# Moving the weights and the tiles of tokens of the projection of k and v to other offsets in SBUF

## The chip, the core and the metric

The kernel runs on one core of one Trainium2 chip. The metric is the device time of one execution in microseconds; three runs of the kernel before gave 2835.35 to 2835.84 us, with a median of 2835.64. The engines named are PE (TensorE, the matrix products) with PEld (its loads of the stationary operand), DVE (VectorE), ACT (ScalarE), POOL (GpSimd) and SP (SyncE, which here only issues transfers).

## The reference

One block of a perceiver: cross-attention to a long context, self-attention with rotary positions, and a feed-forward part with 4-bit weights, each added to its input. What the change touches is the projection of the context to keys and values, over all 8192 context tokens.

```python
def _L0_xattn_ref(x, cond, Wq, bq, Wkv, bkv, Wp, bp):
    B, N, C = x.shape                                   # C = 1024, 16 heads of 64
    q = (x @ Wq + bq).reshape(1, B * N, H, hd)          # 512 queries
    kv = (cond @ Wkv + bkv).reshape(1, -1, 2, H, hd)    # 8192 tokens, 1024 -> 2048
    k, v = (kv[:, :, 0], kv[:, :, 1])
    ...
    q = _fq_sym(q, axis=-1)
    k = _fq_sym(k, axis=-1)
    v = _fq_sym(v, axis=2)
    attn = softmax(q k^T), quantised
    return attn v @ Wp + bp

x = x + _L0_xattn_ref(_layernorm(x), ctx_2048, ...)
x = x + _L0_attn_ref(_layernorm(x), ...)
x = x + _L0_ffn_ref(_layernorm(x), ...)
```

Because k, v and q are rounded to 8 bits, the projection needs nearly all the precision of float32.

## The kernel before

**The products.** A float32 number is split into three tiles of the type float32r: h (high part), l (low part, for weights scaled up) and d (a combination of both). The product of tokens and weights is then h·h and l·l into one PSUM tile `kv_a`, and d·d into another, `kv_b` (`project`, lines 345 to 357). For each tile of 128 tokens there are two halves of 512 output columns, eight blocks k of 128 input channels and three products: 48 matmuls. The tokens are the stationary operand (`lhsT`, 128 x 128, which PEld loads) and the weights the moving one (`rhs`, 128 x 512). Each matmul is preceded by its own load of tokens, and in the trace that load starts 2 to 4 ns after the matmul before has started. The order is fixed: for each half, k from 0 to 7, and in each k the products h, l, d.

**The passes.** There are 64 tiles of tokens, gone through twice: first for v (weights `w3[1]`, s = 0 to 63), then for k (`w3[0]`, s = 64 to 127), 6144 matmuls in all. Beside the pass for v, DVE and ACT also expand the 4-bit weights of the feed-forward part; beside the pass for k, values and keys are quantised and stored. Most of the order of the work is written out by hand: `do(step, function, ...)` puts a function at a step and `perform` issues them in the order of the steps; the middle of the pass for v is a plain loop, which the framework's own scheduler orders. After both passes come the attention to the context (scores, exponentials, values), self-attention, the feed-forward products (line 169 for gate and up, line 1533 for down), all with the same split into h, l and d where float32 precision is needed.

**The tiles.** The weights are 24 tiles of 128 partitions x 1024 numbers (4096 bytes a partition): eight each of `w_h`, `w_l` and `w_d`, in the pool `kv_w` (`weight_hi`, line 240). The tokens of tile s are three tiles of 4096 bytes, `c_h`, `c_l` and `c_d` (`tokens_hi`, line 334), in three sets by s % 3: sets 0 and 2 lie in the pool `early` (`kv_early`), set 1 in the pool `pools["c"]` (`kv_c`). The tiles `bq` (line 277) and `xn` (line 281) of the projection of q use the same places as `c_l2` and `c_h2` before these are needed.

**The addresses.** A pool's places are laid out one after another, in the order in which the program first asks for them, in whole 32 bytes. `kv_w` begins on the left with a tile of 32 bytes at byte 17,024, so the weights begin at 17,056: `w_h` 17,056, 21,152, ..., then `w_l` from 49,824 and `w_d` from 82,592, all 4096 apart and all at 160 modulo 512. After them come three rows of biases (2048 bytes each) and `kv_c` from 121,504: set 1 lies at 160 modulo 512 too. `kv_early` lies on the right and ends at 212,704. Its eleven places of 4096 bytes are `vmax` (167,648), two of `c_raw`, two of `w_raw`, `c_l2` (188,128), `c_h2` (192,224), `c_h0`, `c_l0`, `c_d0` and `c_d2` (208,608): all at 224 modulo 512. A block k of the tokens is 512 bytes further, and the second half of the weights 2048 bytes, so neither changes the place modulo 512.

In the later stages the operands lie as follows, modulo 512: line 1160 has weights (moving) at 448 and stationary tiles at 480; line 1318 moving at 480 and stationary at 448; line 169 moving at 480 and stationary at 128; line 1533 moving at 128 and stationary h, l, d at 160, 160, 128 for the first quarter of a half and at 288, 288, 128 from then on.

Before the change:

Of the kernel before, what the change touches and what calls it, by code (L numbers as in the profile page):

```python
# [34 lines left out]
F32 = mybir.dt.float32  # L35
# [4 lines left out]
F32R = mybir.dt.float32r  # L40
# [6 lines left out]
P = 128  # L47
B, S, C = 4, 128, 1024
NT = B * S // P
NC = C // P  # L50
# [25 lines left out]
REST = (NI - 8 * WHOLE) // 2  # L76
EARLY = 8

LOWEST = -3.0e38
F16_UNITS = 16777216.0  # L80
UP = 4096.0
# [5 lines left out]
def tile_perceiver(  # L87
# [44 lines left out]
    def layernorm(pool, xt, xn, parts=1):  # L132
        st = pool.tile([P, 2, nc.vector.BN_STATS_DIM], F32, name="ln_st", tag="ln_st", bufs=2)
        for i in range(2):
            nc.vector.bn_stats(st[:, i, :], xt[:, ts(i, 512)])
        mv = pool.tile([P, 2], F32, name="ln_mv", tag="ln_mv", bufs=2)
        nc.vector.bn_aggr(mv, st)
        rstd = pool.tile([P, 1], F32, name="ln_rstd", tag="ln_rstd", bufs=2)
        nc.vector.tensor_scalar_add(rstd, mv[:, 1:2], 1e-5)
        nc.scalar.activation(rstd, rstd, AF.Sqrt)  # L140
        nc.vector.reciprocal(rstd, rstd)
        for i in range(parts):
            cols = ts(i, C // parts)
            nc.vector.tensor_scalar(
                xn[:, cols], xt[:, cols], mv[:, 0:1], rstd, ALU.subtract, ALU.mult
            )
# [11 lines left out]
    def split_hi(src, hi):  # L158
        nc.scalar.mul(hi, src, 1.0 - 0.5 / UP)  # L159
# [48 lines left out]
    early = early_s.enter_context(tc.tile_pool(name="kv_early", bufs=2, side="right"))  # L208
# [3 lines left out]
    kv_w = kvstack.enter_context(tc.tile_pool(name="kv_w", bufs=1))  # L212
# [18 lines left out]
    raws, tokens, accs, fs = {}, {}, {}, {}  # L231
# [7 lines left out]

    def weight_hi(i, k):  # L240
        w3[i].append(
            [kv_w.tile([P, C], F32R, name=f"w_{n}", tag=f"w_{n}", bufs=NC) for n in "hld"]
        )
        split_hi(raws["w", i, k], w3[i][k][0])

# [15 lines left out]
    xts, xns, xnTs, qps, qns, wqs, bqs, xpts = {}, {}, {}, {}, {}, {}, {}, {}  # L261
# [12 lines left out]
        queue.dma_start(out=wqs[n, k], in_=wq_src[:, k, ts(n, 512)])  # L274

    def load_bq():
        bqs[0] = early.tile([P, C], F32, name="bq", tag="c_l2", bufs=1)
        nc.sync.dma_start(out=bqs[0], in_=xbq.partition_broadcast(P))

    def norm_of_x(t):  # L280
        xns[t] = early.tile([P, C], F32, name=f"xn{t}", tag="c_h2", bufs=1)
        layernorm(q_t, xts.pop(t), xns[t], parts=2 if t == 0 else 1)

    def transposes_of_x(t):
# [41 lines left out]
    raws, tokens, accs, fs = {}, {}, {}, {}  # L326
# [7 lines left out]
    def tokens_hi(s):  # L334

        pool = pools["c"] if s % 3 == 1 else early
        tokens[s] = [
            pool.tile([P, NC, P], F32R, name=f"c_{n}", tag=f"c_{n}{s % 3}", bufs=1) for n in "hld"
        ]
        split_hi(raws[s], tokens[s][0])  # L340

    def tokens_lo(s):
# [109 lines left out]
    for k in range(NC):  # L452
        do(0.1 if k < 3 else 0.3, load_wq, 0, k)
        do(0.65 if k == 0 else 30, load_wq, 1, k)
    do(0.2, load_x_of_q, 1)
    do(0.45, load_bq)
    do(0.5, load_x_of_q, 2)
    do(0.55, load_x_of_q, 3)
# [3 lines left out]
    for t, at in enumerate((4, 9, 16.4, 24.5)):  # L462
        do(at, norm_of_x, t)
        at = first[t] - (1.6 if t == 0 else 1.9)
        do(at, transposes_of_x, t)
        do(at + 0.1, copies_of_x, t)
        for n, q_at in enumerate(((19, 27.5, 33, 40.9)[t], (48.7, 54.1, 61, 67.5)[t])):
            for k in range(NC):
                do((first, second)[n][t] + 0.88 * k, project_q, n, t, k)
            do(q_at, quantise_q, n, t)  # L470
            do(q_at + 3.1, transpose_q, n, t)
            do(q_at + 8.5, store_q, n, t)
    for k, (raw, hi, lo) in enumerate(
        (
            (0.4, 12.8, 13),
            (0.6, 19.5, 22),
            (16.5, 24, 30.4),
            (24.6, 34, 36),
            (33, 37.5, 38.4),
            (38.5, 42, 43.8),  # L480
            (41, 49.5, 51.6),
            (46.3, 55, 57),
        )
    ):
        do(raw, weight_raw, 1, k)
        do(hi, weight_hi, 1, k)
        do(lo, weight_lo, 1, k)
        do(lo + 2.6, weight_up, 1, k)
    for n in range(2):
        do(27.6, load_tokens, n)  # L490
        do(40, kv_bias, 1, n)
    do(45, tokens_hi, 0)
    do(46.2, tokens_lo, 0)
    do(48.8, load_tokens, 2)
    do(60, lambda: nc.sync.dma_start(out=shifts, in_=nibbles))
    at = 67.4
    for s in range(2):
        for n in range(2):
            for k in range(NC):
                do(at + 11.2 * s + 5.6 * n + 0.7 * k, project, s, n, k)  # L500
    do(at - 0.05, open_pools)
    do(at + 1.5, tokens_hi, 1)
    do(at + 3.2, tokens_lo, 1)
    do(at + 3.3, load_tokens, 3)
    do(at + 6, join, 0, 0)
    do(at + 6.3, tokens_hi, 2)
    do(at + 7.5, tokens_lo, 2)
    do(at + 7.6, load_tokens, 4)
# [177 lines left out]
    for k in range(NC):  # L686
        do(at + (k if k < 4 else 4 * k - 10), weight_raw, 0, k)
        do(at + 4 * k + 4.1, weight_hi, 0, k)
        do(at + 4 * k + 5.7, weight_lo, 0, k)
        do(at + (9.6, 13.4, 17.6, 22.8, 26.6, 30.4, 35, 38.6)[k], weight_up, 0, k)  # L690
# [13 lines left out]
    for u in range(KT):  # L704
        at = TILE * (KT + u)
        s = KT + u
# [50 lines left out]
    with tc.tile_pool(name="at_e", bufs=1) as at_e, tc.tile_pool(  # L757
        name="at_s", bufs=4
    ) as small, tc.tile_pool(name="at", bufs=2) as at, tc.tile_pool(
        name="at_ps", bufs=3, space=PSUM  # L760
# [32 lines left out]
        def scores(n, g):  # L793
# [10 lines left out]
            for i in range(2):  # L804
# [12 lines left out]
                scale=1.0,  # L817
                scalar=LOWEST,
                op0=ALU.mult,
# [4 lines left out]
        def maximum(n):  # L824
# [8 lines left out]
                scale=sqs[:, 1, t, h : h + 1],  # L833
                scalar=-LOWEST,
                op0=ALU.add,
# [174 lines left out]
        with tc.manual_schedule():  # L1010
            for s in range(n_steps + LAG_V):
                n, g = divmod(s, NSC)
# [9 lines left out]
                if n < len(units):  # L1022
                    h, t = units[n]
# [316 lines left out]
    with tc.manual_schedule():  # L1340
# [10 lines left out]
        for h, (w, n) in enumerate(PARTS):  # L1351
            s = PART * h
# [72 lines left out]
        s = PART * len(PARTS)  # L1425
# [12 lines left out]
    with tc.tile_pool(name="ff_t", bufs=2) as ff_t, tc.tile_pool(  # L1438
        name="ff_a", bufs=1
# [36 lines left out]
        with tc.tile_pool(name="ff_g", bufs=2) as ff_g:  # L1476
# [13 lines left out]
            with tc.tile_pool(name="g_ps", bufs=2, space=PSUM) as g_ps, tc.tile_pool(  # L1490
                name="u_ps", bufs=2, space=PSUM
# [17 lines left out]
        with tc.tile_pool(name="ff_h", bufs=1) as ff_h, tc.tile_pool(  # L1509
            name="y_ps", bufs=1, space=PSUM  # L1510
# [135 lines left out]
```

## Time and profile before

| | |
|---|---|
| median of 3 runs | 2835.64 us (2835.35 to 2835.84) |
| profiled execution, first to last instruction | 2844.0 us, 8.4 us above that median |
| mean granted clock of PE | 0.984; 1.00 from 0 to 1350 us |
| PE busy | 2655.8 us, 93% |
| PEld busy | 2060.8 us, 72% |
| DVE busy | 2417.0 us, 85% |
| ACT busy | 1264.9 us, 44% |
| POOL busy | 461.0 us, 16% |
| matmuls of line 351 | 6144, from 66.6 to 1489.2 us |
| one of them, start to end | 387 ns at least, median 393 |
| one load of tokens for them | median 188 ns |

The profile is of one execution; of its time outside the span only the difference to the median is known, and that is negative, so the profile itself costs something. A group's line gives the source line, the engine and operation, the tiles written and read, the shapes, how many there were, their busy time, the mean length of one, and the idle time ahead of them. Matmuls are pipelined, so a group's busy time counts overlap once, while the mean length of one contains it. The view by windows gives for each stretch its length, then for each engine its busy time and how many instructions fall in it, the granted clock (1.00 is full speed), the busy share of the transfers and their rate. The timeline gives for every instruction its start and its length in us.

### The profile page before, as it was taken

The page shows a single profiled execution, that of the slowest core. Times are in us where ns is not written, and L with a number is a line of the kernel's source. Part 1 is how long each engine was busy: PE and PEld are TensorE (multiplying, and loading weights), DVE is VectorE, ACT ScalarE, POOL GpSimd, SP SyncE. Part 2 cuts the span into 40 slices and gives each one's busy share as a digit, 9 for nine tenths or more (in the row PEclk, how much of TensorE's full clock was granted, in tenths as well). Part 3 has the DMA queues.
Part 4 walks back from the last instruction along what each step waited for, and adds up shares of the span by engine and source line. Part 5 has one row for each costly group of instructions (what it writes and reads, how often), then busy time and mean ns, then how long its engine had stood idle before and what let it go on. Part 6 is the DMA issues. An engine that isn't in the chain of part 4 may idle for free.

```text
span 2844.0 us, 41119 instructions
## 1 busy us (share of the span) xinstructions
PE 2655.8 (93%) x15496; PEld 2060.8 (72%) x15496; DVE 2417.0 (85%) x3963; ACT 1264.9 (44%) x1404; POOL 461.0 (16%) x615
## 2 busy tenths in 40 slices
PE   9999999999999999999997877778778899999998
PEld 4888888888888888888874555555555687788887
DVE  7999998555799988888879999999996898776684
ACT  4111121211323333333218999999994244333332
POOL 0111111000012222222122332233312000000000
PEclk9999999999999999999998999999999999999999
DMA  6655565222447776767436898887874221122222
GB/s 198 207 197 195 192 210 200 89 98 95 137 127 202 192 192 182 194 183 188 124 88 143 164 165 164 155 162 152 168 142 146 86 80 61 52 97 97 96 90 96
DMA packets 450327, 412.66 MB, mean 145 GB/s; under 512 B 354888, under 2 KB 359560, under 8 KB 450128
## 3 DMA queue, kind: packets, MB, share of 16 engines
q1 hardware_dynamic: 401984, 249.86, 36.4%
q0 software_dynamic: 47088, 159.12, 17.4%
q8 instruction: 122, 2.00, 0.3%
q10 hardware_dynamic: 1056, 1.05, 0.2%
q14 instruction: 77, 0.63, 0.1%
HBM read 220.14 MB, written 104.34 MB: 114 GB/s over the span
## 4 chain that ended last, share of the span: by engine, by line
PE 73%; DVE 19%; issue 4%; ACT 2%; DMA 1%; POOL 0%; DVEq 0%; SPq 0%; ACTq 0%; POOLq 0%
PE kv_a L351 33%; PE kv_b L351 17%; DVE e L813 14%; PE acc_a L1160 3%; PE gate_a L169 3%; PE up_a L169 3%; PE y_a L1533 3%; PE q_ps L301 2%; PE acc_b L1160 1%; PE up_b L169 1%; PE gate_b L169 1%; PE y_b L1533 1%; PE a_pt L862 1%; PE sc L806 1%; DVE sw_l L162 1%
## 5 line engine op out<-in xcount | busy, mean ns | idle before, releaser
L351 PE MATMUL kv_a<-w_h,c_h 128*128 128x512 f32 x2048 | 806.4, 394 | 0.0
L351 PE MATMUL kv_a<-w_l,c_l 128*128 128x512 f32 x2048 | 806.0, 394 | 0.2 <-ACT w_l L250 0.2
L351 PE MATMUL kv_b<-w_d,c_d 128*128 128x512 f32 x2048 | 806.1, 394 | 0.0
L813 DVE CUSTOM_DVE_ANT_0 e<-sc,sk 128x1024 f32<-128x1024 f32 x512 | 593.7, 1219 | 14.0 <-PE sc L806 13.0
L847 ACT ACTIVATE a<-e,m,sqs 128x4096 int16<-128x4096 f32 x128 | 490.4, 3831 | 25.4 <-DVE m L829 21.9
L351 PEld LDWEIGHTS kv_a<-w_l,c_l 128*128 128x128 f32 x2048 | 384.8, 188 | 89.6 <-ACT w_l L250 0.6
L351 PEld LDWEIGHTS kv_a<-w_h,c_h 128*128 128x128 f32 x2048 | 384.9, 188 | 88.9 <-issue 0.2
L351 PEld LDWEIGHTS kv_b<-w_d,c_d 128*128 128x128 f32 x2048 | 384.8, 188 | 89.0 <-DVE c_d L163 0.3
L159 ACT ACTIVATE c_h<-c_raw 128x1024 fp32r<-128x1024 f32 x128 | 135.5, 1059 | 463.8 <-PE kv_a L351 454.3
L365 DVE SCALAR_TENSOR_TENSOR f<-kv_a,bkv 128x512 f32<-128x512 f32 x256 | 175.8, 687 | 167.0 <-PE kv_a L351 166.3
L806 PE MATMUL sc<-kt,qT 64*128 64x512 bf16 x1024 | 207.6, 398 | 95.0 <-DVE mx L813 93.6
L604 ACT CAST kst<-kT 128x512 bf16<-128x512 int16 x128 | 89.5, 700 | 300.1 <-DMA kT<-ki 300.0
L862 PE MATMUL a_pt<-ident,a 128*128 128x128 f32 x1024 | 177.6, 299 | 25.2 <-ACT a L847 21.0
L366 DVE SCALAR_TENSOR_TENSOR f<-kv_b,f 128x512 f32<-128x512 f32 x256 | 176.7, 690 | 19.0
L786 POOL PARTITION_BROADCAST sk<-sk_row x120 | 142.5, 1298 | 308.2 <-DVE mx L813 308.1
L862 PEld LDWEIGHTS a_pt<-ident,a 128*128 128x128 f32 x1024 | 113.5, 147 | 92.1 <-ACT a L847 51.8
L162 DVE TENSOR_TENSOR fw_l<-fw_raw,fw_h 128x1024 fp32r<-128x1024 f32 x64 | 78.3, 1224 | 99.4 <-ACT fw_h L159 99.3
L806 PEld LDWEIGHTS <-qT 64*128 64x128 bf16 x1024 | 71.6, 93 | 124.1 <-issue 94.2
L162 DVE TENSOR_TENSOR c_l<-c_raw,c_h 128x1024 fp32r<-128x1024 f32 x128 | 155.6, 1216 | 6.6 <-ACT c_h L159 6.1
L163 DVE SCALAR_TENSOR_TENSOR c_d<-c_l,c_raw 128x1024 fp32r<-128x1024 f32 x128 | 156.3, 1221 | 2.3
L159 ACT ACTIVATE fw_h<-fw_raw 128x1024 fp32r<-128x1024 f32 x64 | 67.9, 1061 | 175.0 <-PE y_a L1533 71.5
L571 ACT CAST vq<-vi 128x1024 f16<-128x1024 int16 x64 | 67.1, 1049 | 174.0 <-DVE vi L564 137.1
(214 smaller groups left out, 4121.0 us busy)
## 6 DMA issues: line engine op xcount, KB each, us to landing
c_raw<-in_ctxT SPq DMA_DIRECT2D x128, 512.0 KB, 3.6
v_d<-f POOLq DMA_DIRECT2D x64, 512.0 KB, 3.1
vl<-v_d POOLq DMA_DIRECT2D x64, 512.0 KB, 4.3
gu_d<-w_ffn POOLq DMA_DIRECT2D x44, 512.0 KB, 3.1
fw_raw<-gu_d SPq DMA_DIRECT2D x42, 512.0 KB, 3.2
k_d<-kst POOLq DMA_DIRECT2D x128, 128.0 KB, 3.4
vq_d<-vq POOLq DMA_DIRECT2D x32, 512.0 KB, 5.0
kt<-k_d SPq DMA_DIRECT2D x64, 256.0 KB, 3.8
```

What stands on the lines that cost most here:

```text
L159: nc.scalar.mul(hi, src, 1.0 - 0.5 / UP)
L162: nc.vector.tensor_tensor(lo, src, hi, ALU.subtract)
L163: nc.vector.scalar_tensor_tensor(df, lo, -1.0 - UP, src, ALU.mult, ALU.add)
L169: nc.tensor.matmul(ps, lhsT=lhs(i, k), rhs=rhs(i, k), start=(k == 0 and i != 1), stop=(k == NC - 1 and i != 0),)
L351: nc.tensor.matmul(ps, lhsT=tokens[s][i][:, k, :], rhs=w3[s < KT][k][i][:, ts(n, 512)], start=(k == 0 and i != 1), stop=(k == NC - 1 and i ...
L365: nc.vector.scalar_tensor_tensor(f, a, 1.0 + 1.0 / UP, bias[s < KT][n], ALU.mult, ALU.add)
L366: nc.vector.scalar_tensor_tensor(f, b, -1.0 / UP, f, ALU.mult, ALU.add)
L786: nc.gpsimd.partition_broadcast(tile_of_scales(h, g), sks_at[h][32 * c : 32 * c + 1, ts(half, SC)], channels=P)
L806: nc.tensor.matmul(ps[:, ts(i, 512)], lhsT=qT[rows, h, ts(t, P)], rhs=kts[h, g // 2][rows, ts(g % 2, 512)], start=True, stop=True,)
L813: nc.vector.tensor_tensor_reduce(out=state[n]["e"][-1][:, ts(g % (NSC // NEC), SC)], in0=ps, in1=sks_at[h, g], scale=1.0, scalar=LOWEST, o ...
L847: nc.scalar.activation(a, st["e"][c], AF.Exp, bias=st["m"], scale=sqs[:, 0, t, h : h + 1], accum_out=sums[h][:, t, c : c + 1],)
L862: nc.tensor.transpose(pt[:, i, :], a[:, at_word + P * i : at_word + P * i + P], ident)
```

## The change

The weights' tiles get eight more numbers (32 bytes) per partition, of which the products use the first 1024. The tiles of tokens, and `bq` and `xn`, which share their places, get 72 more numbers in `kv_early` and 16 more in `kv_c`; and the tokens begin inside their tile at a word given by `STARTS` for the set (s % 3) and the part (h, l, d). Number, order and size of all instructions stay.

```diff
+PADS = (72, 16)
+STARTS = ((0, 8, 64), (4, 12, 0), (64, 72, 16))
...
     def weight_hi(i, k):
         w3[i].append(
-            [kv_w.tile([P, C], F32R, name=f"w_{n}", tag=f"w_{n}", bufs=NC) for n in "hld"]
+            [
+                kv_w.tile([P, C + 8], F32R, name=f"w_{n}", tag=f"w_{n}", bufs=NC)[:, :C]
+                for n in "hld"
+            ]
         )
...
-        bqs[0] = early.tile([P, C], F32, name="bq", tag="c_l2", bufs=1)
+        bqs[0] = early.tile([P, C + PADS[0]], F32, name="bq", tag="c_l2", bufs=1)[:, :C]
...
-        xns[t] = early.tile([P, C], F32, name=f"xn{t}", tag="c_h2", bufs=1)
+        xns[t] = early.tile([P, C + PADS[0]], F32, name=f"xn{t}", tag="c_h2", bufs=1)[:, :C]
...
     def tokens_hi(s):
 
         pool = pools["c"] if s % 3 == 1 else early
-        tokens[s] = [
-            pool.tile([P, NC, P], F32R, name=f"c_{n}", tag=f"c_{n}{s % 3}", bufs=1) for n in "hld"
-        ]
+        tokens[s] = []
+        for i, n in enumerate("hld"):
+            pad = PADS[s % 3 == 1]
+            tile_ = pool.tile([P, C + pad], F32R, name=f"c_{n}", tag=f"c_{n}{s % 3}", bufs=1)
+            at_word = STARTS[s % 3][i]
+            tokens[s].append(tile_[:, at_word : at_word + C].rearrange("p (k q) -> p k q", q=P))
         split_hi(raws[s], tokens[s][0])
```

## The prediction

> **What bounds the kernel now.** I read the share of the engines first, then the chain of work that ended last, then the costliest groups.
>
> ```profile
> span 2844.0 us, 41119 instructions
> ...
> PE 73%; DVE 19%; issue 4%; ACT 2%; DMA 1%; POOL 0%; DVEq 0%; SPq 0%; ACTq 0%; POOLq 0%
> ...
> L351 PE MATMUL kv_a<-w_h,c_h 128*128 128x512 f32 x2048 | 806.4, 394 | 0.0
> L351 PE MATMUL kv_a<-w_l,c_l 128*128 128x512 f32 x2048 | 806.0, 394 | 0.2 <-ACT w_l L250 0.2
> L351 PE MATMUL kv_b<-w_d,c_d 128*128 128x512 f32 x2048 | 806.1, 394 | 0.0
> ```
>
> The 6144 matmuls of line 351 hold the chain from 66.6 to 1489.2 us and wait for nothing. The 394 ns is a length with overlap; what counts is the step from one start to the next. The view by windows, over whole tiles of tokens, gives that step (the counts hold one or two matmuls of the neighbour; a tile is 48):
>
> ```profile
> core 0: us, PE busy (x) PEld busy (x), PEclk, DMA share, GB/s
> 288.98:311.37 22.39, 22.39 (x97) 18.04 (x96) 1.00 0.58 206
> 311.37:322.28 10.91, 10.91 (x49) 9.01 (x48) 1.00 0.51 193
> 322.28:344.68 22.40, 22.40 (x98) 18.05 (x96) 1.00 0.52 182
> 344.68:355.59 10.91, 10.91 (x50) 9.01 (x49) 1.00 0.59 216
> ```
>
> Two tiles take 22.39 us, 233.2 ns a step; the third takes 10.91, 227.3 ns a step; then again. The granted clock is 1.00 in all four. The slower two are the sets of tokens with s % 3 of 2 and 0, in kv_early; the faster is set 1, in kv_c. Only addresses tell them apart: weights lie at 160 modulo 512, set 1 at 160 too, sets 0 and 2 at 224. Inside set 1 the steps settle at about 226.7:
>
> ```profile
> 319.79 0.39 PE L351 MATMUL kv_a<-w_l,c_l 128*128 128x512 f32 x1
> 320.01 0.39 PE L351 MATMUL kv_b<-w_d,c_d 128*128 128x512 f32 x1
> 320.24 0.39 PE L351 MATMUL kv_a<-w_h,c_h 128*128 128x512 f32 x1
> 320.47 0.39 PE L351 MATMUL kv_a<-w_l,c_l 128*128 128x512 f32 x1
> 320.69 0.39 PE L351 MATMUL kv_b<-w_d,c_d 128*128 128x512 f32 x1
> 320.92 0.39 PE L351 MATMUL kv_a<-w_h,c_h 128*128 128x512 f32 x1
> ```
>
> Five steps in 1.13 us. While a matmul streams a weights tile, the tokens of the next are loaded; so I take as variable the distance: offset of the next matmul's tokens less offset of this one's weights, modulo 512. Set 1 has 0, sets 0 and 2 have 64. Later stages, by their addresses, add more:
>
> ```profile
> core 0: us, PE busy (x) PEld busy (x), PEclk, DMA share, GB/s
> 2500.46:2523.79 23.33, 23.33 (x101) 18.77 (x100) 1.00 0.31 107
> ...
> 2735.50:2763.23 27.73, 27.73 (x122) 22.54 (x121) 1.00 0.28 96
> ```
>
> The gate and up products (line 169) have 160 throughout: 23.33/100 = 233.3. The products of line 1160 have 32 and those of line 1318 have 480; starts a few matmuls apart in their timelines give 233 there as well. The down products (line 1533) repeat the distances 160, 160, 0: 27.73 us over 120 steps is 231.1, just (2 x 233.3 + 226.7)/3. So four distances other than 0 cost one and the same step, and 0 saves 6.7 ns even standing alone. Earlier in line 1533 the repeat is 32, 0, 32 and a step is 231.9, so mixing can cost 0.8 more.
>
> **The change part by part.** *Weights.* A tile grows by 32 bytes, so the eight of a name lie 32 apart: w_h and w_d at 160 to 384, w_l at 416 round to 128. *Tokens.* Six tiles of kv_early grow by 288 bytes, three of kv_c by 64. kv_early ends at byte 212,704 and grows downwards by 1728; kv_c is moved up by 24 x 32 = 768. With the starts inside, h, l and d lie at 96, 416, 416 (set 0), 432, 16, 32 (set 1), 64, 320, 0 (set 2). Over eight k and three products a set has 24 distances. Of the 72, four are 0 (one, one and two in sets 0, 1, 2); 14 are among 32, 64, 160 and 480; 54 are at distances that no row shows, 16 of them, all in set 1, at odd multiples of 16.
>
> *The step.* Before: 4074 steps beside sets 0 and 2 at 233.3 are 950.5 us, 2059 beside set 1 at 227.3 are 468.0; together 1418.5 over 6133 (the few that wait are left out), a mean of 231.3. For an unseen distance the low end is the fastest step that any row keeps up, 226.7, and nothing but the absence of rows excludes less; the high end is the slowest single step, about 239 (line 1533). I take 233.3: four of four distances that are not 0 have it, on both sides of 0 (480 is -32) and with either tile at several offsets. After: 6133 x 233.3 = 1430.8, less 6133 x 4/72 x 6.7 = 2.3 for the zeros: 1428.5, or **+10.0**. Mixed distances cost between 0 and 6133 x 0.8 = 4.9 by the two stretches of line 1533; I take 2. Sum **+12**, against the profiled execution's 2844.0, which is 8.4 over the median of 2835.64; a difference in PE's steps carries over to either.
>
> *All else is taken at nothing.* Instructions, their shapes and their order stay: views of 1024 elements in longer rows. The splits do not feel the offset: line 162 takes 1206 to 1226 ns over all its tiles, those at 160 and those at 224. bq and xn share tags with c_l2 and c_h2 and are only moved. c_raw lands 3.6 us after issue, tiles ahead; any loss there is covered by PE's 11 us a tile. The keys' tiles of the attention, opened during the last tile of tokens, now lie over other old tiles, some of set 0 where they had been over set 2. Those are read out when the last tile begins, 11 us before PE needs keys, so no wait; uncovered, a load is 3.8 us. A slower PE delays ACT, DVE and the queues by as much and gives each more slack.
>
> *A rule against the change.* Rows: 227.3 and 233.2 for the same shapes at one clock. The Trainium skill, "TensorE: Matmul & The Clock Gate", Step-by-step: what each phase is for, says of PE's two read ports: "Loading the next tile's weights doesn't steal SBUF read bandwidth from the running matmul." By it offsets would be worth nothing and the time would stay at 2835.6; the rows differ, and I go by them. The same page, Back-to-back issue gap, puts 512 columns at N / 2.4 + 2.5 = 215.8 ns, and an estimate from it, were every collision gone, is 6133 x (231.3 - 215.8) = 95 us less; no run here shows such a step.
>
> **The rivals.** *Unseen distances are cheap (faster).* If 0 is no isolated dip and the 54 unseen pairs run at 226.7, PE gains 6133 x 54/72 x 6.7 = 30.8 against 1428.5: 1397.7, -20.8, about 2815. For it: three quarters of the pairs are unseen. Against: both neighbours of 0, a near and a far distance, are equal. It decides once the mean step falls under 231.3, that is once some 22 of the 54 run at 226.7. DVE caps it in part, for it is nearly full while the feed-forward weights are expanded, and 5.2 us of 300 is all that PE could gain there:
>
> ```profile
> 150.00:300.00 150.00, 150.00 (x651) 121.86 (x650) 148.01 (x340) 27.76 (x27) 21.67 (x37) 1.00 0.54 195
> 300.00:450.00 150.00, 150.00 (x650) 121.86 (x649) 146.78 (x244) 29.71 (x28) 26.59 (x39) 1.00 0.59 210
> ```
>
> *Offsets are not the cause, or the period is shorter (no change).* If the pool makes set 1 fast, nothing moves: 2836. Against: line 1533 follows its offsets inside one stage. With a period of 128, ten further pairs count as zeros: 6133 x 10/72 x 6.7 = 5.7 less, 2842, at the edge of no change. *Odd starts or mixing cost extra (slower still).* If the 16 pairs of set 1 at odd multiples of 16 take 240 ns, that is 2059 x 16/24 x 6.7 = 9.2; with full mixing (2.9 more than taken) about 2860. Nothing in the trace shows such a start under a matmul of this kind.
>
> **How the numbers follow.** A fair measurement tells 0.2%, 5.7 us, from no change. The forecast has 0.57, its own range 2843 to 2853. Slower still has 0.13, no change 0.08, faster 0.22. Faster by over 0.2% is thus 0.22, within 0.08, slower 0.70. The range reaches to 2862 above (0.06 left out) and to 2818 below, leaving out about 0.12.
>
> **What would show it.** Right: tiles of set 1 at 11.2 us like the others, no third tile at 10.91; the down products unchanged at 231.1; DVE's busy time unchanged, its idle time longer. In the timeline four pairs in 72 stay near 227, and those name the distance 0. Wrong: if tiles of sets 0 and 2 fall under 11.1 us, unseen distances are cheap; if set 1 alone exceeds 11.3, odd starts cost; if set 1 stays at 10.91, the offset was never the cause.

## The result and the profile after

The changed kernel takes 2843.52 us (median of 10 runs, 2840.78 to 2848.04) against 2836.97 of the kernel before (10 runs, 2833.85 to 2839.90): a ratio of 1.0020, 95% interval 1.0011 to 1.0029, so 3 to 8 us slower. 12 us more than 2835.64 had been forecast, about 2848, with a range of 2818 to 2862.

Engines, chain and costliest groups, from the page of the changed kernel (`project` is now line 359):

```profile
span 2838.9 us, 41119 instructions
...
PE 71%; DVE 21%; issue 5%; ACT 2%; DMA 1%; POOL 0%; DVEq 0%; SPq 0%; POOLq 0%; ACTq 0%
...
L359 PE MATMUL kv_b<-w_d,c_d 128*128 128x512 f32 x2048 | 809.9, 395 | 0.0
L359 PE MATMUL kv_a<-w_l,c_l 128*128 128x512 f32 x2048 | 807.6, 394 | 0.2 <-ACT w_l L255 0.2
L359 PE MATMUL kv_a<-w_h,c_h 128*128 128x512 f32 x2048 | 805.8, 393 | 0.0
```

The three groups still wait for next to nothing (0.2 us), and the names at the head of the chain are the same. Their mean lengths, 393 to 395 ns, tell nothing of the change, because they contain the overlap; the step from start to start has to be read from windows. Here are three tiles of tokens of the second pass, sets 0, 1 and 2 in this order, first before and then after (columns: stretch and its length, PE and PEld busy with their counts, granted clock, share of the transfers, GB/s):

```profile
1067.10:1078.30 11.20, 11.20 (x50) 9.02 (x48) 1.00 0.71 180
1078.30:1089.21 10.91, 10.91 (x50) 9.01 (x49) 1.00 0.63 168
1089.21:1100.41 11.20, 11.20 (x50) 9.02 (x49) 1.00 0.85 229
```

```profile
1072.28:1083.40 11.12, 11.12 (x50) 9.01 (x48) 1.00 0.67 162
1083.40:1094.54 11.14, 11.14 (x49) 9.01 (x48) 1.00 0.63 168
1094.54:1105.72 11.18, 11.18 (x49) 9.02 (x48) 1.00 0.87 220
```

A tile is 48 steps. Set 1 loses the most, from 10.91 to 11.14 us (227.3 to 232.1 ns a step). Sets 0 and 2 gain a little, 233.3 to 231.7 and 232.9. Over all 6134 steps that don't wait (6133 before), the mean is 232.24 ns where it was 231.29.

From the first to the last start the projection takes 1428.2 us instead of 1422.5. **These 5.7 us are the whole of the change**, within what the runs can tell. That the profiled execution is nevertheless shorter than the one before (2838.9 against 2844.0) lies mostly in the attention, which takes 655.1 us from its first score to its last product with the values before and 646.5 after. In the same stretch of it the granted clock was 0.95 before and 0.99 after; whether that is the cause is not shown. The tiles of the keys there do move with the change, by 960 bytes, but two kernels below move them too, by 64 bytes, and their medians differ from before by what their projection differs (24.9 of 24.9 us, and 12.5 of 12.4). So I put the long attention down to that one execution. The 8.4 us by which it exceeds its median are no price of profiling as such either: the changed kernel's profiled execution took 2840.78 us for a span of 2838.9.

```profile
1650.00:1800.00 150.00, 117.67 (x1422) 81.95 (x1421) 143.79 (x281) 141.60 (x121) 47.43 (x54) 0.95 0.87 159
```

```profile
1650.00:1800.00 150.00, 118.55 (x1470) 82.87 (x1469) 148.46 (x291) 145.74 (x123) 49.70 (x56) 0.99 0.83 165
```

So below, stages are compared by their own windows, and spans are not. What should have stayed did: the gate and up products take 23.33 us for 100 steps (lines 169 and 171), and the down products 27.72 us for 120 (27.73 before):

```profile
2495.30:2518.63 23.33, 23.33 (x102) 18.76 (x101) 1.00 0.29 105
...
2730.34:2758.06 27.72, 27.72 (x121) 22.53 (x121) 1.00 0.28 95
```

### The profile page after: what moved, and what is told of

Read it like the earlier page. It is cut to its first block, busy times and chain, and to the rows that moved or that the text cites. A ratio compares the mean times of both kernels' runs of the same rounds, so it can differ in the third digit from the quotient of the medians.

```text
span 2838.9 us, 41119 instructions
## 1 busy us (share of the span) xinstructions
PE 2650.6 (93%) x15496; PEld 2051.6 (72%) x15496; DVE 2416.5 (85%) x3963; ACT 1263.3 (44%) x1404; POOL 462.5 (16%) x615
## 4 chain that ended last, share of the span: by engine, by line
PE 71%; DVE 21%; issue 5%; ACT 2%; DMA 1%; POOL 0%; DVEq 0%; SPq 0%; POOLq 0%; ACTq 0%
PE kv_a L359 33%; PE kv_b L359 17%; DVE e L821 15%; PE up_a L171 3%; PE gate_a L171 3%; PE y_a L1541 3%; PE acc_a L1168 3%; PE up_b L171 1%; PE gate_b L171 1%; PE y_b L1541 1%; PE acc_b L1168 1%; PE q_ps L306 1%; DVE sw_l L164 1%; PE a_pt L870 1%; PE sc L814 1%
## 5 line engine op out<-in xcount | busy, mean ns | idle before, releaser
L164 DVE TENSOR_TENSOR c_l<-c_raw,c_h 128x1024 fp32r<-128x1024 f32 x128 | 155.8, 1218 | 5.8 <-ACT c_h L161 5.5
```

The lines of the kernel that those rows point to most:

```text
L164: nc.vector.tensor_tensor(lo, src, hi, ALU.subtract)
```

## The experiments

The word "distance" is the prediction's: the offset of the next matmul's tokens less that of this one's weights. All kernels below but the last version leave everything outside the projection alone, but for tiles that shift along with its pools, and none leaves out any work. Times are compared with the kernel before as run beside them on the same chip; steps are from the starts in the trace.

### Every distance 0, and every distance 64

The first tile of `kv_w` made 64 bytes longer moves the weights and set 1 to 224 modulo 512, where sets 0 and 2 already lie:

```diff
-    shifts = kv_w.tile([P, 2], I32, name="shifts")
+    shifts = kv_w.tile([P, 18], I32, name="shifts")[:, :2]
```

> The kernel before with its small first tile 64 bytes longer, so that the weights and set 1 lie at 224 modulo 512 like sets 0 and 2: every distance is 0. If the distance sets the step (theory A: 0 is cheap wherever the tiles lie; theory B, each distance has its own price, says the same here), all three sets take 226.7 to 227.3 ns a step and the projection loses 4074 x 6.0 = 24 us; where the expansion of the feed-forward weights fills VectorE up to 2 of these are lost: about 2812 to 2816. If the pool or the region of set 1 makes it fast (theory C), sets 0 and 2 stay at 233.3 and the time at 2836.

The opposite moves set 1 alone, by 64 bytes inside `kv_c` (a longer `c_h1` whose tokens start 16 words in):

```diff
+PADS = ((0, 0, 0), (16, 0, 0), (0, 0, 0))
+STARTS = ((0, 0, 0), (16, 0, 0), (0, 0, 0))
...
+            pad, at_word = PADS[s % 3][i], STARTS[s % 3][i]
+            tile_ = pool.tile([P, C + pad], F32R, name=f"c_{n}", tag=f"c_{n}{s % 3}", bufs=1)
+            tokens[s].append(tile_[:, at_word : at_word + C].rearrange("p (k q) -> p k q", q=P))
```

> The kernel before with set 1 moved by 64 bytes inside its pool, to 224: every distance is 64. Theories A and B: set 1 rises from 227.3 to 233.3 ns a step like the others, 2059 x 6.0 = 12.4 us more, about 2849. Theory C (the pool): set 1 stays at 227.3 and the time at 2836.

Three tiles as above, sets 0, 1, 2; first the kernel with every distance 0, then the one with every distance 64:

```profile
1053.00:1063.88 10.88, 10.88 (x49) 9.01 (x48) 1.00 0.71 184
1063.88:1074.76 10.88, 10.88 (x49) 9.01 (x48) 1.00 0.63 168
1074.76:1085.64 10.88, 10.88 (x49) 9.01 (x48) 1.00 0.89 216
```

```profile
1080.27:1091.46 11.19, 11.19 (x49) 8.97 (x48) 1.00 0.67 173
1091.46:1102.66 11.20, 11.20 (x49) 8.98 (x48) 1.00 0.67 170
1102.66:1113.87 11.21, 11.21 (x50) 8.98 (x49) 1.00 0.85 216
```

All sets at 226.7, or all at 233.3, whichever pool they lie in: addresses make the difference and pools do not. It is also the relation that counts and not the tokens' own place: tokens at 224 take 233.3 beside weights at 160 and 226.7 beside weights at 224. 64 bytes in one tile bring 2813.91 us against 2838.81 (ratio 0.9908, 0.9891 to 0.9924), and the projection takes 1397.7 us, 24.9 less. With every distance 64 it is 2851.27 (1.0044, 1.0029 to 1.0059). VectorE's ceiling in the first pass was reached but held PE up nowhere in it: of the 300 us from 150 on DVE was busy for 299.19, and PE started 26 more matmuls there than before (1327 against 1301). Some 28.4 us were saved in steps, and 3.5 of them went to waits of PE early in the second pass: its steps of over 260 ns add up to 7.5 us where they were 4.0, the longest (2.4 us) while a transpose waits for DVE.

```profile
150.00:300.00 150.00, 150.00 (x663) 124.20 (x662) 150.00 (x345) 29.78 (x28) 22.22 (x38) 1.00 0.57 198
300.00:450.00 150.00, 150.00 (x664) 124.20 (x663) 149.19 (x253) 28.72 (x27) 33.47 (x40) 1.00 0.61 213
```

### The change's two parts alone

The weights alone, with the changed kernel's padding and starts of the tokens set to nothing:

```diff
-PADS = (72, 16)
-STARTS = ((0, 8, 64), (4, 12, 0), (64, 72, 16))
+PADS = (0, 0)
+STARTS = ((0, 0, 0), (0, 0, 0), (0, 0, 0))
```

> The change's weights alone: a weight tile is 32 bytes longer, tokens without padding and without starts of their own (sets 0 and 2 at 224, set 1 at 416, whose tiles follow the weights). Distances run through multiples of 32 with k and are all even multiples of 16. Theory A: no pair but the few at 0 is cheap, 233 ns a step in all three sets, about 2848, unless mixing itself saves steps. Theory B: the mean over the distances' own prices, as in the changed kernel some 232 ns, about 2843.

The tokens alone, with the changed kernel's weights as before:

```diff
-                kv_w.tile([P, C + 8], F32R, name=f"w_{n}", tag=f"w_{n}", bufs=NC)[:, :C]
+                kv_w.tile([P, C], F32R, name=f"w_{n}", tag=f"w_{n}", bufs=NC)
```

> The change's tokens alone: weights at 160 throughout, tokens padded and started as in the change. Each set repeats three distances (set 0: 256, 256, 448; set 1: 112, 128, 16; set 2: 160, 352, 416, for the pairs to l, to d and to the next h), none of them 0. Theory A: 233.3 ns in all sets, 2849. Theory B: sets differ among themselves, each the mean of its three prices; no number can be had from the rows so far. If odd multiples of 16 cost extra, set 1 is the slowest.

| | step of set 0, 1, 2 (ns) | projection (us) | time beside before (us) | ratio, interval |
|---|---|---|---|---|
| before | 233.3, 227.3, 233.3 | 1422.5 | | |
| weights alone | 232.5, 232.5, 232.6 | 1429.7 | 2846.74 and 2838.81 | 1.0024, 1.0014 to 1.0034 |
| tokens alone | 230.9, 232.4, 231.3 | 1424.1 | 2839.99 and 2838.81 | 1.0003, 0.9994 to 1.0012 |
| both: the change | 231.7, 232.1, 232.9 | 1428.2 | 2843.52 and 2836.97 | 1.0020, 1.0011 to 1.0029 |

Spread weights make all sets alike, at 224 and at 416 for the tokens; that alone is 7.2 us of the projection. Tokens at offsets of their own take from set 1 about what they give to sets 0 and 2. Tokens alone never have distance 0 modulo 512 and still stay below 233.3, so the theory that only 0 is cheap is wrong, unless mixing is what saves. That was the next question.

### One distance held at a time

Weights at 160; each set of tokens is brought to one distance by padding, three distances a kernel. The lists of the first kernel, with the code of the kernel for distance 64:

```diff
+PADS = ((0, 0, 64), (64, 0, 0), (64, 0, 48))
+STARTS = ((0, 0, 0), (64, 0, 0), (0, 0, 0))
```

> The kernel before with weights at 160 and each set of tokens at one distance of its own: 128 (set 0), 256 (set 1), 384 (set 2). Theory A (held, every distance but 0 costs the same): 233.3 ns a step in all three sets, some 2850. Theory B (each distance has its own price): the sets differ; since tokens moved alone gave 230.9 in a set with 256, 256 and 448, the distance 256 should then be below 231. A period of 256 would show as set 1 at 226.7, one of 128 as all three at 226.7.

> The same with the distances 16 (set 0), 96 (set 1) and 320 (set 2). Theory A: 233.3 ns a step in all three, and 16 no dearer than 96. Theory B: the sets differ; the single steps of the changed kernel suggest 320 below 230. If the dip at 0 has a width of more than 16 bytes, set 0 stays near 227.

> The same with the distances 48 (set 0), 192 (set 1) and 448 (set 2). Theory A: 233.3 ns a step in all three. Theory B: the sets differ, 448 below 231 by the single steps of tokens alone.

> Weights at 160, one distance held in each set: 480 (set 0), 32 (set 1), 160 (set 2), which so far were seen only in other stages. With a price for each distance and a period of 256, all three are at 233 to 234 ns a step, and the mean of the eight prices is 231.9. If the stage or the shape of the moving operand (lines 169 and 1318 read four separate pieces) matters, they differ from 233.3.

First 128, 256, 384, then 48, 192, 448:

```profile
1066.20:1077.36 11.16, 11.16 (x49) 9.05 (x48) 1.00 0.74 188
1077.36:1088.28 10.92, 10.92 (x49) 9.02 (x48) 1.00 0.60 168
1088.28:1099.44 11.16, 11.16 (x50) 9.05 (x49) 1.00 0.86 209
```

```profile
1065.74:1076.93 11.19, 11.19 (x49) 9.12 (x48) 1.00 0.75 185
1076.93:1087.92 10.99, 10.99 (x50) 9.02 (x48) 1.00 0.67 167
1087.92:1098.91 10.99, 10.99 (x49) 9.02 (x48) 1.00 0.87 197
```

128 and 384 cost the same to 0.2 ns, and so do 192 and 448; 256 settles at 226.7 like 0, after some slow steps at the start of each tile that make its mean 227.4. **The period is 256 bytes and not 512**, nor 128, since 128 costs 232.5 and 0 costs 226.7. All held distances together:

| distance modulo 256 | 0 | 16 | 32 | 48 | 64 | 96 | 128 | 160 | 192 | 224 |
|---|---|---|---|---|---|---|---|---|---|---|
| step, ns | 226.7 | 226.7 or 233.4 | 233.3 | 233.2 | 233.3 | 234.2 | 232.5 | 233.3 | 228.9 | 233.3 |

In the tokens alone, set 0 thus had distance 0 modulo 256 in two pairs of three and still took 230.9, and set 2, with 160, 96 and 160, took 231.3: neither is the mean of its held prices.

The distance 16 has two gaits. Whole tiles run at the one or the other, mostly in turn, with the same addresses of both operands throughout; here two tiles of set 0 of that kernel, 33 us apart (10.88 and 11.21 us for 48 steps):

```profile
1042.97:1053.85 10.88, 10.88 (x49) 9.01 (x48) 1.00 0.70 184
1076.29:1087.50 11.21, 11.21 (x50) 9.08 (x49) 1.00 0.67 165
```

So something counts beside the addresses of the two operands. The PSUM tiles written also alternate from one tile of this set to the next, but they do not decide it: s = 60 and s = 66 write the same four and take 226.7 and 233.2 ns a step. That it is the state in which a tile begins is a guess. The kernels took 2836.84, 2845.56 and 2834.62 us against 2841.41 (the fourth 2847.88 against 2840.03), one run each, too few to compare by; their steps are what they were run for.

### Known distances, mixed

Three distances that cost 233 when held, within one set:

```diff
+PADS = ((104, 48, 0), (16, 24, 0), (24, 104, 104))
+STARTS = ((0, 0, 0), (8, 0, 0), (0, 0, 0))
```

> Only distances that cost 233.3 when held, but mixed within a set: 480, 160, 64 (set 0), 64, 160, 32 (set 1), 64, 160, 480 (set 2), for the pairs to l, to d and to the next h. Theory B: a mean of equal prices, 233.3 ns in all three sets. Theory A with mixing as the cause of the saving: below 233.3, about 231 to 232.5 as in the sets of tokens alone, and different for the two orders of the same distances (sets 0 and 2) if it is the order that counts.

```profile
1068.57:1079.66 11.09, 11.09 (x50) 9.02 (x48) 1.00 0.68 169
1079.66:1090.64 10.98, 10.98 (x49) 9.02 (x48) 1.00 0.58 161
1090.64:1101.84 11.20, 11.20 (x50) 9.03 (x48) 1.00 0.86 221
```

Over all their tiles the sets take 231.1, 228.9 and 233.2 ns (2834.24 us against 2841.41, one run). Sets 0 and 2 have the same three distances in two orders and differ by 2.2 ns. A price for each distance, summed, is wrong too: mixing can save, and the order decides how much.

### Is it the next tokens, or a matmul's own operands?

The weights h, l, d at 160, 224 and 352, by two small gaps; set 0 at its own product's weights, set 1 at those of the product before, set 2 at 224:

```diff
...
+        w3[i].append([])
+        for n in "hld":
+            w3[i][k].append(kv_w.tile([P, C], F32R, name=f"w_{n}", tag=f"w_{n}", bufs=NC))
+            if i == 1 and k == 0 and n != "d":
+                kv_w.tile([P, 16 if n == "h" else 32], F32, name=f"gap_{n}", tag=f"gap_{n}", bufs=1)
...
+PADS = ((16, 32, 96), (16, 16, 0), (112, 0, 0))
```

> Weights h, l, d at 160, 224, 352. Tokens of set 0 lie where the weights of their own product lie, tokens of set 1 where the weights of the product before lie (modulo 256), set 2 at 224 throughout. If the weights being streamed collide with the load of the next tokens, set 1 falls to 226.7 ns a step and set 0, whose next distances are 64, 128 and 64, stays at 231 to 233.3. If a matmul's own two operands matter, it is the other way round: set 0 at 226.7, set 1 at 231 to 233.3.

The same with gaps of 40 and 48 words, which put the weights at 160, 64 and 0 modulo 256:

> As in the run on own and next, but the weights h, l, d lie at 160, 64, 0 modulo 256, so that each product's weights begin 64 or 96 bytes before the last one's instead of 64 or 128 after. Tokens of set 0 lie with their own weights, of set 1 with the weights of the product before, of set 2 at 160 throughout. If what counts is where a stream of weights begins against the one before (sums of three steps then move by whole eighths of a 32-byte turn, 6.7 ns), going backwards saves: some set comes to 224.4 to 226.7 ns a step. If any change of the weights' place costs, all three sets stay at 230 to 233, as in that run.

| step of set, ns | own operands at 0 | next distance 0 | tokens all at one offset |
|---|---|---|---|
| weights at 160, 224, 96 modulo 256 | 230.0 | 233.0 | 230.9 |
| weights at 160, 64, 0 modulo 256 | 231.4 | 232.0 | 233.2 |

Neither. With the next distance 0 at every pair the step is 233.0 (11.19 us for a tile), as dear as a held distance of 64, once the weights' own offset changes from product to product; here three tiles of the first of these kernels, sets 0, 1, 2:

```profile
1068.27:1079.30 11.03, 11.03 (x49) 9.01 (x48) 1.00 0.64 167
1079.30:1090.49 11.19, 11.19 (x50) 9.01 (x49) 1.00 0.64 168
1090.49:1101.57 11.08, 11.08 (x49) 9.01 (x48) 1.00 0.87 223
```

Going backwards saves nothing either. In these runs a set came to 226.7 and stayed there only where its weights have one offset, its tokens have one offset, and the two agree modulo 256 (at 16, in some tiles only). What the rest share is not known. Times were 2833.47 against 2840.03 and 2840.22 against 2838.81, one run each.

### The rule in the other stages

The kernel with every distance 0, and gaps of 32 to 224 bytes in the later stages that bring the float32r products of lines 1160, 1318, 169 and 1533 to distance 0 modulo 256 as well:

```diff
+    sa_p = sa_s.enter_context(tc.tile_pool(name="sa_p", bufs=1))
+    sa_p.tile([P, 8], F32, name="gap_w")
...
+        ff_p.tile([P, 24], F32, name="gap_f")
...
-        ss = ff.tile([P, NT, 2], F32, name="ss")
+        ss = ff.tile([P, 64], F32, name="ss")[:, : 2 * NT].rearrange("p (t n) -> p t n", n=2)
...
+            ff_h.tile([P, 32], F32, name="gap_h")
```

> All distances at 0 as in the run before with that name, and in the later stages too: gaps of 32 to 224 bytes bring lines 1160, 1318, 169 and 1533 to distance 0. If the price of the distance is a matter of the operands and not of this stage, each of these steps falls to 226.7 ns: line 169 by 1008 x 6.7 = 6.7 us, line 1533 by 528 x 4.7 = 2.5, line 1160 by 864 x 6.5 = 5.6 less what its waits for VectorE take back; 9 to 14 us under 2814, about 2802. If it is a matter of the projection alone, nothing is gained over 2814.

The gate and up products over 100 steps, and the down products over 120, in this kernel:

```profile
2468.10:2490.77 22.67, 22.67 (x102) 18.77 (x101) 1.00 0.32 106
...
2697.00:2724.20 27.20, 27.20 (x122) 22.52 (x121) 1.00 0.29 97
```

23.33 us became 22.67 and 27.73 became 27.20: 226.7 ns a step in both. Line 169 is at distance 256 here and not at 0, which shows the period once more. 2803.75 us against 2840.03, a ratio of 0.9876 (0.9859 to 0.9893): 36 us faster than the kernel before, and faster than both kernels of this study. Of that 26.2 are the projection; the gate and up products give 6.7 (234.97 to 228.25 us over all their steps), the down products 2.4 (526 steps from 231.4 to 226.8). In line 1160 the steps between waits fall from 233.2 to 228.6 ns, but the stage takes 273.5 us from its first to its last start, where it took 274.5 before and 271.9 in the kernel with distance 0 in the projection alone: its waits take the gain back.

## Why the prediction was right, and where it was not

**Right: what bounds, and which way it goes.** PE's steps are the time; the projection's 5.7 us reach the end in full. Everything costed at nothing was nothing: DVE is busy for 2416.5 us (2417.0), the split of line 162 (now 164) takes 1218 ns (1216), and the later products keep their steps. Set 1 is where the loss comes from.

**Mis-sized: "I take 233.3".** The three terms of the step (1430.8 less 2.3 plus 2, together 1430.5 us) measured 6133 x 232.24 = 1424.3, 6.2 us less. The 233.3 rested on four distances that all cost 233.3, and these happened to be 32, 64, 160 and 224 modulo 256, all on the plateau. Of the unseen ones, when held, 192 is cheap (228.9), 128 a little (232.5), and 256 is another 0. Sets 0 and 2 gained where I had them stand still, but not by these prices one by one: in the changed kernel the steps with distance 256 have a mean of 233.4. The mean of the eight held prices at multiples of 32 is 231.9, which would have given +3.7 (6133 x (231.9 - 231.3)). That the sum came out above 231.3 is in part luck: set 1, which had the shortest step of all, lost 10.0 us, but sets 0 and 2 gave back 4.2 of them, and with the tokens moved alone nearly all (the projection grew by 1.6 us).

**Wrong: the period.** I took offsets modulo 512 as the variable and gave a shorter period one sentence, with 128. The rows could not tell 256 from 512, since no two of the distances they held lay 256 apart. The run with 128, 256 and 384 settled it.

**Wrong: "0 saves 6.7 ns even standing alone".** The four pairs in 72 do not stand out: over the steps with distance 0 in the changed kernel the mean is 230.7, and single steps run from 224 to 243 all over a tile. In line 1533 the sum (2 x 233.3 + 226.7)/3 fitted, but the runs with changing offsets show that prices of pairs do not add up, so the fit was no proof. The trace before showed as much. In the last stretch of line 1533 the steps with distance 0 have a mean of 230.9 ns and the others 231.2, where the sum needs 226.7 and 233.3; here the steps from l to d (distance 0) are 0.23 us like the rest:

```profile
2739.05 0.39 PE L1533 MATMUL y_a<-fw_l,h_l 128*128 128x512 f32 x1
2739.28 0.39 PE L1533 MATMUL y_b<-fw_d,h_d 128*128 128x512 f32 x1
2739.51 0.39 PE L1533 MATMUL y_a<-fw_h,h_h 128*128 128x512 f32 x1
2739.74 0.39 PE L1533 MATMUL y_a<-fw_l,h_l 128*128 128x512 f32 x1
2739.97 0.39 PE L1533 MATMUL y_b<-fw_d,h_d 128*128 128x512 f32 x1
```

The wish that these pairs would name the distance 0 was not fulfilled.

**Mixing, taken at +2.** Its sign depends on the order: in the run with known distances it saved from nothing to 4.4 ns a step. With spread weights it cost 0.6 (232.5 against the 231.9 of the held prices).

**The rivals.** *Offsets are not the cause* fell with the two runs at 0 and at 64. *Unseen distances are cheap* was half right: some are when held, and the loss is 5.7 and not 12, but the mean step did not get under 231.3. How much of the difference is cheap distances and how much is mixing cannot be told apart, since the prices do not add up. *Odd starts cost extra* fell: 16 and 48 held are no dearer than 32 or 64 (other odd multiples were not held), and set 1 is not the slowest set of the changed kernel.

**The rule set against the rows.** The Trainium skill, "TensorE: Matmul & The Clock Gate", Step-by-step: what each phase is for, says that a load of weights takes no read bandwidth from the running matmul. These runs do not isolate the load, but they show that where the two operands lie is worth 24.9 us in one stage, against a sentence by which it would be worth nothing. The same page's 215.8 ns for 512 columns, which its section Back-to-back issue gap gives for an isolated matmul, was reached by no held arrangement; the shortest here is 226.7.

**Open.** Why 226.7 and 233.3, and what turns one into the other. Some sums over a repeating pattern come in a fixed unit: a step of 226.7 is 34 times 6.67 ns, one of 233.3 is 35 times, and the threes of the mixed set 1 (226, 231, 230) sum to 103 times. The held 128 (232.5, 34.9 times) and 96 (234.2, 35.1 times) do not fit so simply. It looks like a turn of fixed length into which each stream has to fall, and two gaits at one address would fit that, but it is only argued. A matmul without a load beside it was not tried.

## What to carry to other kernels

In a long run of float32r products of this shape (128 x 128 stationary, 128 x 512 moving, a load before each), let all moving tiles begin at one offset modulo 256 bytes, all stationary tiles at one offset, and make the two equal: here 64 bytes brought 25 us in one stage, and four gaps of 32 to 224 bytes in the later stages made it 36 in all. Read such effects from the step between starts over whole tiles, since the mean length of a matmul hides them. When a handful of rows all show one price, ask which residues they cover before the rest is put at the same price.

## What was not expected

A layout can settle into either of two gaits at the same addresses (distance 16: 10.88 or 11.21 us a tile, mostly in turn). The step did not follow the load on the other engines: in the first pass, with DVE full, and in the second, with other transfers, a held arrangement kept its step (at distance 0, 226.67 ns in all three sets of the first pass, and 226.7 in the tiles of the second that do not wait). And the order of the same three distances is worth 2.2 ns a step.
